# A graph layer on one core: where edge lists, the last chunk's attention and the experts' first rows stand in the queues

## The chip, the core and the metric

The kernel runs on one core of one Trainium2 chip. The metric is device time in microseconds (us): the median over runs of one compiled program. The profile is one further execution of the same program, taken by the hardware profiler. Names of engines: PE is TensorE, DVE VectorE, ACT ScalarE, POOL GpSimd, SP SyncE (it only issues transfers).

## What is computed

10,000 nodes with 512 features, 160,000 edges sorted by destination, all in float32:

```python
xn = layernorm(x)
h = relu(segment_sum((xn @ W)[src] * edge_weight[:, None], dst) + bias)
q, k, v = split(xn @ w_qkv.T)            # 8 heads of 64
q = softmax(q, over the head) * 64**-0.5
k = softmax(k, over all nodes)
context = k.T @ v                        # per head, 64 x 64
mix = layernorm((q @ context) @ w_out.T) * gamma
x = x + h + mix
xn = layernorm(x)
p = softmax(mean(xn) @ router.T)         # the top two of 11 set the weights of 6 experts
x = x + sum_e weight_e * (gelu(xn @ W1[e] + b1[e]) @ W2[e] + b2[e])
```

## The kernel before

The nodes go in 20 chunks: 19 of 512 rows (128 partitions by SUB = 4 rows) and a last one of 272 (68 partitions). The edges go in 1,250 tiles of 128; a group of four or eight tiles is gathered, weighted by a selection matrix and summed into one 128-row part.

PE's order is written out by hand. The orders of the other engines are made by a scheduler from the order of the code, the dependencies and a model of durations; within an engine, and within SP's line of transfers, that order is then fixed, so an instruction that waits holds all behind it. `behind(inst, other)` (L157) adds nothing but an edge for that scheduler.

Stages, in order of time:

1. Rows. `normal_rows` (L411) loads a chunk of `x` on SP, takes statistics on DVE, finishes them on POOL, scales on ACT and stores the normalised rows to `xn_d` from ACT. The first two chunks (KEPT) stay in SBUF; the others go through seven buffers (`a_io`). When LISTS = 10 chunks are normalised, the code asks for the four edge lists (`edges_listed`, L445) and begins `place_edges` (L454), a generator of some fifteen passes on DVE over the lists that works out each edge's place in its window. Two of its steps are taken after each further chunk, the rest at L858. Beside this PE works on the keys and queries of the first two chunks (EARLY = 2); `rows_of` (L830) reloads later chunks from `xn_d`, the first time for chunk 2.
2. Keys and edges. For each chunk, keys, queries and the context (`seven`, L246, and L911), with edge groups put in between. POOL gathers the messages (`edges_in`, L573: one indirect transfer of 256 KB per tile, 24 buffers), PE sums them (`edges_summed`, L595), ACT copies the sum out and stores it to `part_d`. `work` (L698) counts the time of PE's own products and calls for one tile per PACE = 0.9 us of it. POOL also adds parts of neighbouring windows in DRAM (`carry`, L672).
3. Rows again (L1062 to L1122). For chunk c: `attention` (L1038) of chunk c + 3 (loads `queries_in`, `rows_again`; products `po`; row statistics), the sums of the edges `gathered` (L1013, one indirect transfer on POOL) and transposed into `aT`, then the products `pg` and the rest of the row, stored to `x1_d`. The edge groups go on at one tile per ROW_PACE = 0.96 us; `far_enough` (L996) forces those that a chunk needs, with LEAD = 10 groups more. At c = 17 (NCH - 3) `all_edges_in` (L1005) sums what is left, closes the edges' buffers and asks for the experts' weights (`experts_weights`, L293); the attention of the last chunk, whose loads were issued at c = 16 and kept in `held["last"]`, comes after that. At c = 18 the rows of the experts' first chunk are asked for (`rows_in`, L315: four transfers), scaled on ACT (`normalising`, L341: 16 instructions) with statistics brought in place by `stats_of_squares` (L331, the product `pst`), transposed on DVE (`rows_turned`) and summed (`turned_in`).
4. Experts (L1370 to L1394): `hidden` and `rows_out` for 20 chunks, with products `px`, `py`, `pz`. A last branch, for more than four experts, is not taken with these inputs.

Of the kernel before, what the change touches and what calls it, by code (L numbers as in the profile page):

```python
# [9 lines left out]
F32 = mybir.dt.float32  # L10
# [17 lines left out]
FAR = 1.0e5  # L28
EARLY = 2
ROWS_IN = 1.6  # L30
LISTS = 10
CHECKED = 5
KEPT = 2
PRODUCT = 0.83
PACE = 0.9
ROW_PACE = 0.96
LATE = 4
MIXED = 3

# [3 lines left out]
CARRIES = [0, CHAINED] + [w for _, w in AT_HAND]  # L43
FIXED = 2
LAG = 16
LEAD = 10
LAG_ROWS = 10
AHEAD = 16
NORM2 = 7.0
# [7 lines left out]
def gps_layer_kernel(  # L57
# [41 lines left out]
    def tokens(t, c):  # L99
        b, r = chunks[c]  # L100
        return t[b : b + r * SUB, :].rearrange("(p s) d -> p s d", s=SUB)
# [55 lines left out]
    def behind(inst, other):  # L157

        tc.add_manual_dep(inst.ins, other.ins.name, mybir.DependencyInfo(
            mybir.DependencyClass.NoSync, mybir.DependencyReason.SCHED_ONLY), reason="order of work")  # L160
# [27 lines left out]
    def softmax_rows(q, r, s):  # L188

        q3 = q[:r, s, :].rearrange("p (h e) -> p h e", e=HEAD)  # L190
        qs = small.tile([P, D // HEAD], F32, name="qs")
        nc.vector.tensor_reduce(qs[:r], q3, axis=AX.X, op=ALU.add)
        nc.vector.reciprocal(qs[:r], qs[:r])
        nc.vector.tensor_tensor(q3, q3, qs[:r, :, None].to_broadcast([r, D // HEAD, HEAD]), ALU.mult)

    def transposed(o, t, r, psum, tag, by_act=(1, 3)):

# [190 lines left out]
    with ExitStack() as ph:  # L388
# [16 lines left out]


        normal = []
        placing = []
        last_stats = [None]

        def normal_rows(n):  # L411

            for c in range(len(normal), min(len(normal) + n, NCH)):
                r = chunks[c][1]
                xt = (xp if c < KEPT else a_io).tile([P, SUB, D], F32, name="xn")
                nc.sync.dma_start(xt[:r], tokens(x, c))
                mv = small.tile([P, SUB, 2], F32, name="mv")
                last_stats[0] = row_stats(xt, r, mv, on_pool=True)
                nc.gpsimd.tensor_tensor(mv[:r, :, 0], mv[:r, :, 0], mv[:r, :, 1], ALU.mult)
                nc.gpsimd.tensor_scalar(mv[:r, :, 0], mv[:r, :, 0], -1.0, None, op0=ALU.mult)  # L420
                for i in range(SUB):
                    nc.scalar.activation(xt[:r, i, :], xt[:r, i, :], AF.Identity,
                                         bias=mv[:r, i, 0:1], scale=mv[:r, i, 1:2])
                nc.scalar.dma_start(tokens(xn_d, c), xt[:r])
                normal.append(xt)
                if len(normal) == LISTS:
                    placing.append(place_edges(*edges_listed()))
                for _ in range(2 if placing else 0):
                    next(placing[0], None)

        zero = tmp.tile([P, D], F32, name="zero")
        nc.vector.memset(zero, 0.0)
# [21 lines left out]
        def place_edges(dst_sb, row_sb):  # L454


            nc.vector.tensor_scalar(row_sb, row_sb, 2, None, op0=ALU.arith_shift_right)
            yield
            nc.vector.memset(bases[:, 0:1], 0.0)
            nc.vector.memset(bases[:, NW:], FAR)  # L460
            nc.vector.tensor_copy(bases[:, 1:PAIRED],
# [34 lines left out]
            yield  # L496
            by_window_of(beyond, nodes, good, ALU.mult)
            yield
            nc.vector.scalar_tensor_tensor(place, place, float(SUB), good, op0=ALU.add, op1=ALU.subtract)
            yield  # L500
            nc.vector.scalar_tensor_tensor(good, place, float(SUB), beyond, op0=ALU.is_lt, op1=ALU.is_equal)
            yield
            nc.vector.scalar_tensor_tensor(good, place, float(WIN), good, op0=ALU.is_lt, op1=ALU.mult,
# [69 lines left out]
        def edges_in(i):  # L573

            t0, batch = tiles_of(i)
            n = min(GROUP * batch, NET - t0)
            m = [None] * n
            for j in range(batch):
                for h in range(GROUP):
                    k = h * batch + j  # L580
                    if k < n:
                        m[k] = pools["m"].tile([P, D], F32, name="msg")
                        nc.gpsimd.indirect_dma_start(  # L583
                            out=m[k], out_offset=None, in_=xn_d,
                            in_offset=bass.IndirectOffsetOnAxis(ap=src_sb[:, t0 + k : t0 + k + 1], axis=0))
            sel = pools["w"].tile([P, 2 * GROUP, WIN], F32, name="sel", bufs=6)
            if n < GROUP * batch:
                nc.vector.memset(sel[:, n:, :], 0.0)
            nc.vector.tensor_tensor(sel[:, :n], iota_w[:, None, :].to_broadcast([P, n, WIN]),  # L589
                                    place[:, t0 : t0 + n, None].to_broadcast([P, n, WIN]), ALU.is_equal)  # L590
            nc.vector.tensor_tensor(sel[:, :n], sel[:, :n],
                                    w_sb[:, t0 : t0 + n, None].to_broadcast([P, n, WIN]), ALU.mult)
            return batch, m, sel
# [236 lines left out]
        def rows_of(c):  # L830
            if c < KEPT:
                return normal[c]
            xn = xp.tile([P, SUB, D], F32, name="xn")
            nc.sync.dma_start(xn[: chunks[c][1]], tokens(xn_d, c))
            return xn

        def turned_rows(c, xn):
# [4 lines left out]
        def finish(o, ek, r, at):  # L842
            if o is ek:
                nc.vector.tensor_tensor(kacc[:r], kacc[:r], ek[:r, at, :], ALU.add)
            else:
                softmax_rows(o, r, at)

        wk = kvp.tile([P, KB, D], F32, name="wk")
        nc.sync.dma_start(wk, w_qkv_t[:, D : 2 * D].rearrange("(k p) d -> p k d", p=P))
# [5 lines left out]
        xnT = turned_rows(0, xn)  # L855
        for c, (_, r) in enumerate(chunks):
            if c == EARLY:
                for _ in placing[0]:  # L858
                    pass
                norm_ctx.close()  # L860
                pools["w"] = edge_ctx.enter_context(tc.tile_pool(name="edge_w", bufs=3))
                done[1] = -16 * PACE
                pools["m"] = edge_ctx.enter_context(tc.tile_pool(name="edge_m", bufs=24,
                                                                 reuse_waits="tile"))
# [37 lines left out]
                        finish(qt, ek, r, q)  # L902
            if c + 1 == EARLY:
                normal_rows(NCH)
                xn_next = rows_of(c + 1)
            if c + 1 < NCH:
                xnT = turned_rows(c + 1, xn_next)
# [97 lines left out]
        def all_edges_in():  # L1005
            edges_to(NQ)
            carry(CARRIES[-1], NW - 1)
            assert not carried
            pools.clear()
            edge_ctx.close()  # L1010
            experts_weights()

        def gathered(c):  # L1013
            r = chunks[c][1]
            n_rows = far_enough(c)
            at = io.tile([P, SUB, D], F32, name="at", tag="at" if c < NCH - 1 else "qT")
            nc.gpsimd.indirect_dma_start(
                out=at[:r].rearrange("p s d -> p (s d)"), out_offset=None, in_=by_four[: n_rows // SUB, :],
                in_offset=bass.IndirectOffsetOnAxis(ap=row_of[:r, c : c + 1], axis=0))
            return at  # L1020

        def queries_in(c):
            qT = io.tile([P, KB, SUB * P], F32, name="qT")
            nc.sync.dma_start(qT[:, :, : SUB * chunks[c][1]], qT_d[c])
            return qT

        def rows_again(c):
            xt = io.tile([P, SUB, D], F32, name="xt", bufs=1)
            nc.sync.dma_start(xt[: chunks[c][1]], tokens(x, c))
            return xt  # L1030
# [7 lines left out]
        def attention(c, beside):  # L1038


            r = chunks[c][1]
            qT, xt = held.pop("last") if c == NCH - 1 else (queries_in(c), rows_again(c))
            ot = io.tile([P, SUB, D], F32, name="ot", bufs=MIXED + 2)
            for s in range(SUB):
                if s == SUB - 1:
# [17 lines left out]
        for c, (_, r) in enumerate(chunks):  # L1063
# [2 lines left out]

            if c == NCH - 3:
                all_edges_in()
                ats += [gathered(c + 1), gathered(c + 2)]

            def nodes_rows():
                transposed(aT, at, r, psum, "ps", by_act=range(KB))

            if c + MIXED < NCH - 1:
                mixed.append(attention(c + MIXED, nodes_rows))
            elif c == NCH - 3:
                mixed.append(attention(NCH - 1, nodes_rows))
            else:
                nodes_rows()
            if c < NCH - 3:  # L1080
                ats.append(gathered(c + 1))
            if c == NCH - 4:
                held["last"] = queries_in(NCH - 1), rows_again(NCH - 1)

            for s in range(SUB):
                po = psum.tile([P, D], F32, name="pg", tag="ps")
# [20 lines left out]
            if c == NCH - 3:  # L1107
                sums_of_weights()
            if c == NCH - 2:
                io_f["in"] = ctx.enter_context(tc.tile_pool(name="f_in", bufs=1, reuse_waits="tile"))  # L1110

                io_f["squares"] = io_f["in"].tile([P, P // SQ, P], F32, name="squares")
                for b in range(P // SQ):
                    nc.vector.tensor_copy(
                        io_f["squares"][:, b].rearrange("k (g t) -> k g t", t=SQ),
                        ident[:, None, b * SQ : (b + 1) * SQ].to_broadcast([P, P // SQ, SQ]))
                xn = rows_in(0)
                st = small.tile([P, P // SQ, 1, SUB, 2], F32, name="st_sq", bufs=1)
                stats_of_squares(st, 0)
                for step in normalising(0, xn, st[:, :, 0]):  # L1120
                    step()
                turn = turned_in(0, rows_turned(0, xn))  # L1122
        in_order.close()
        query_ctx.close()

# [347 lines left out]
```

## Time and profile before

| what | value |
|---|---|
| median of 4 runs | 3517.76 us |
| lowest, highest | 3502.45, 3531.32 us |
| the profiled execution's own time | 3520.93 us |
| its span | 3519.2 us |
| PE busy | 3264.1 us, 93% of the span |
| PEld (weight loads) busy | 1918.3 us, 55% |
| DVE busy | 1766.5 us, 50% |
| ACT busy | 830.9 us, 24% |
| POOL busy | 1320.4 us, 38% |
| mean granted clock of PE | 0.964 |

The span is the time from the first to the last instruction of the profiled execution; 1.7 us of its own time lie around it. Busy time is the time in which an engine had an instruction running; a wait is given with what ended it (its releaser), as far as the trace shows one, and "issue" where it shows none. The granted clock is the share of PE's full clock that it was given.

### The profile page before, as it was taken

The numbers are of one execution on the slowest core, as the hardware profiler recorded it, in microseconds if no ns is written. First come the engines' busy times: TensorE is split into PE (matmuls) and PEld (weight loads), VectorE is DVE, ScalarE is ACT, GpSimd is POOL, SyncE is SP. The second block draws the span as 40 slices with busy tenths as digits, with TensorE's granted clock in tenths as the row PEclk, the third lists the DMA queues.
The fourth block names the chain that finished last, engine by engine and source line by source line (L and its number), as shares of the span: only waits on it lengthen the run. The fifth ranks groups of instructions, "written<-read, shape, count | busy, mean of one in ns | idle before, by whom it ended". The sixth has DMA issues, their size and how long they took to land. (4 is left out here: it accounts for less than half of the span.)

```text
span 3519.2 us, 36142 instructions
## 1 busy us (share of the span) xinstructions
PE 3264.1 (93%) x12819; PEld 1918.3 (55%) x12819; DVE 1766.5 (50%) x3902; ACT 830.9 (24%) x1674; POOL 1320.4 (38%) x1421
## 2 busy tenths in 40 slices
PE   6899998988989879998989987999999999999998
PEld 3343433333333333333333335888888888888886
DVE  6644545453444425555655566545445544544542
ACT  5321212121211112221212113222222222222221
POOL 3466666666666657666766730000000000000000
PEclk9999999999999979999999999999999999999999
DMA  9677777877777878898999892221212212122111
GB/s 389 236 224 247 228 247 243 262 218 222 229 219 240 253 260 317 300 321 294 336 309 318 302 265 63 60 72 60 60 48 84 56 52 84 49 60 72 60 37 38
DMA packets 216735, 654.39 MB, mean 186 GB/s; under 512 B 34425, under 2 KB 74361, under 8 KB 188831
## 3 DMA queue, kind: packets, MB, share of 16 engines
q0 software_dynamic: 104096, 354.29, 32.3%
q1 hardware_dynamic: 69992, 175.33, 15.2%
q10 hardware_dynamic: 42452, 122.31, 9.0%
q8 instruction: 105, 1.72, 0.2%
q14 instruction: 90, 0.74, 0.1%
HBM read 491.21 MB, written 166.63 MB: 187 GB/s over the span
## 5 line engine op out<-in xcount | busy, mean ns | idle before, releaser
L583 POOL DMA_INDIRECT msg<-xn_d,src_sb x1250 | 1239.3, 991 | 614.0 <-issue 285.1
L601 PE MATMUL pm<-msg,sel 128*32 128x512 f32 x2504 | 350.5, 613 | 40.0 <-issue 29.2
L911 PE MATMUL pc<-xn,ek 128*128 128x512 f32 (+1 forms) x640 | 311.2, 632 | 23.2 <-issue 17.5
L209 PE MATMUL pg<-wq,aT 128*128 128x512 f32 (+1 forms) x640 | 305.6, 622 | 19.8 <-issue 18.3
L209 PE MATMUL po<-G,qT 128*128 128x512 f32 (+1 forms) x640 | 302.4, 615 | 8.6 <-issue 7.9
L604 ACT COPY part<-pm 128x512 f32<-128x512 f32 x217 | 127.0, 586 | 723.1 <-remote 258.1
L209 PEld LDWEIGHTS pg<-wq,aT 128*128 128x128 f32 (+1 forms) x640 | 117.9, 193 | 208.0 <-issue 192.8
L601 PEld LDWEIGHTS pm<-msg,sel 128*32 128x32 f32 x2504 | 66.6, 109 | 290.1 <-issue 252.4
L911 PEld LDWEIGHTS pc<-xn,ek 128*128 128x128 f32 (+1 forms) x640 | 124.0, 201 | 183.3 <-issue 170.8
L209 PEld LDWEIGHTS po<-G,qT 128*128 128x128 f32 (+1 forms) x640 | 117.6, 192 | 184.5 <-issue 176.4
L243 PE MATMUL px<-xnT,w_sb 128*128 128x256 f32 (+1 forms) x800 | 203.9, 378 | 6.7 <-DVE u L1290 6.5
L166 DVE BATCH_NORM_STATS2 st<-ot 128x6 f32<-128x512 f32 (+1 forms) x160 | 110.3, 690 | 195.9 <-issue 111.4
L243 PE MATMUL p<-kq_sum,xs_b 128*128 128x512 f32 (+1 forms) x432 | 201.9, 600 | 3.3 <-issue 1.9
L243 PE MATMUL px<-w_sb,hh 128*128 128x256 f32 (+1 forms) x800 | 186.4, 380 | 0.0
L243 PE MATMUL py<-xs,w_sum 128*128 128x256 f32 (+1 forms) x800 | 185.9, 375 | 0.0
L243 PE MATMUL p<-wk,xnT 128*128 128x512 f32 (+1 forms) x288 | 149.2, 642 | 36.5 <-issue 29.2
L243 PE MATMUL py<-w_sum,hh 128*128 128x256 f32 (+1 forms) x800 | 179.2, 379 | 0.0
L589 DVE TENSOR_TENSOR sel<-iota_w,place 128x128 f32<-128x128 f32 (+2 forms) x217 | 74.3, 343 | 198.3 <-remote 71.4
L243 PEld LDWEIGHTS px<-xnT,w_sb 128*128 128x128 f32 x800 | 150.2, 191 | 29.7 <-DVE u L1290 10.0
L243 PEld LDWEIGHTS px<-w_sb,hh 128*128 128x128 f32 (+1 forms) x800 | 150.7, 188 | 23.0
L243 PEld LDWEIGHTS py<-w_sum,hh 128*128 128x128 f32 (+1 forms) x800 | 150.0, 188 | 22.7
L243 PEld LDWEIGHTS py<-xs,w_sum 128*128 128x128 f32 x800 | 150.2, 191 | 20.0
(298 smaller groups left out, 4574.2 us busy)
## 6 DMA issues: line engine op xcount, KB each, us to landing
part_d<-part ACTq DMA_DIRECT2D x217, 256.0 KB
msg<-xn_d,src_sb POOLq DMA_INDIRECT x1250
xn<-in_x SPq DMA_DIRECT2D x19, 1024.0 KB
xn_d<-xn ACTq DMA_DIRECT2D x19, 1024.0 KB
qT_d<-qT ACTq DMA_DIRECT2D x19, 1024.0 KB
qT<-qT_d SPq DMA_DIRECT2D x19, 1024.0 KB
xt<-in_x SPq DMA_DIRECT2D x19, 1024.0 KB
x_d<-ot SPq DMA_DIRECT2D x19, 1024.0 KB
```

Of the source, the lines that this page charges most:

```text
L166: nc.vector.bn_stats(st[:r, s, :], t[:r, s, :])
L209: nc.tensor.matmul(po[:r, :], t[:, kb, s * r : (s + 1) * r], w[:, kb, :], start=kb == 0, stop=kb == KB - 1)
L243: nc.tensor.matmul(o, lhs[j], rhs[j], start=start and j == 0, stop=stop and j == n - 1, skip_group_check=True)
L583: nc.gpsimd.indirect_dma_start(out=m[k], out_offset=None, in_=xn_d, in_offset=bass.IndirectOffsetOnAxis(ap=src_sb[:, t0 + k : t0 + k + 1], ...
L589: nc.vector.tensor_tensor(sel[:, :n], iota_w[:, None, :].to_broadcast([P, n, WIN]), place[:, t0 : t0 + n, None].to_broadcast([P, n, WIN]), ...
L601: nc.tensor.matmul(pm[h * WIN : (h + 1) * WIN, :], sel[:, k, :], m[k] if k < len(m) else m[0], start=j == 0, stop=j == batch - 1, skip_gro ...
L604: nc.scalar.copy(part, pm)
L911: nc.tensor.matmul(pc, ek[:r, s, cb * P : (cb + 1) * P], xn[:r, s, :], start=s == 0, stop=s == SUB - 1)
```

## The change

Seven edits in one:

- LISTS goes from 10 to 18; the steps of `place_edges` are no longer taken one by one after each chunk. Its first step is tied behind the last chunk's statistics, and the steps that return an instruction (the first, and the pass at L499) are tied behind the last softmax when the generator is run to its end.
- `rows_of` ties the first reload behind the last load of `x`.
- `gathered` ties the gather of a chunk's sums behind the last message asked for.
- ROW_PACE goes from 0.96 to 0.98, LEAD from 10 to 12.
- The last chunk's attention is no special case any more: it is done at c = 16, with its loads, and `held["last"]` is gone.
- At c = 17, when the edges are in, the experts' rows buffers are opened first, the first chunk's rows are asked for, then the weights.
- The copies `squares` move to the same place.

```diff
-LISTS = 10
+LISTS = 18
-ROW_PACE = 0.96
+ROW_PACE = 0.98
-LEAD = 10
+LEAD = 12
@@ softmax_rows
-        nc.vector.tensor_tensor(q3, q3, qs[:r, :, None].to_broadcast([r, D // HEAD, HEAD]), ALU.mult)
+        return nc.vector.tensor_tensor(q3, q3, qs[:r, :, None].to_broadcast([r, D // HEAD, HEAD]), ALU.mult)
@@ normal_rows
-                nc.sync.dma_start(xt[:r], tokens(x, c))
+                last_load[0] = nc.sync.dma_start(xt[:r], tokens(x, c))
...
-                for _ in range(2 if placing else 0):
-                    next(placing[0], None)
@@ place_edges
-            nc.vector.tensor_scalar(row_sb, row_sb, 2, None, op0=ALU.arith_shift_right)
-            yield
+            yield nc.vector.tensor_scalar(row_sb, row_sb, 2, None, op0=ALU.arith_shift_right)
...
-            nc.vector.scalar_tensor_tensor(place, place, float(SUB), good, op0=ALU.add, op1=ALU.subtract)
-            yield
+            yield nc.vector.scalar_tensor_tensor(place, place, float(SUB), good, op0=ALU.add, op1=ALU.subtract)
@@ edges_in
-                        nc.gpsimd.indirect_dma_start(
+                        held["asked"] = nc.gpsimd.indirect_dma_start(
@@ rows_of
-            nc.sync.dma_start(xn[: chunks[c][1]], tokens(xn_d, c))
+            load = nc.sync.dma_start(xn[: chunks[c][1]], tokens(xn_d, c))
+            if c == KEPT:
+                behind(load, last_load[0])
@@ finish
-                softmax_rows(o, r, at)
+                last_softmax[0] = softmax_rows(o, r, at)
@@ the loop over keys
-                for _ in placing[0]:
-                    pass
+                for step in placing[0]:
+                    if step:
+                        behind(step, last_softmax[0])
...
                 normal_rows(NCH)
+                behind(next(placing[0]), last_stats[0])
@@ all_edges_in
-            experts_weights()
@@ gathered
-            nc.gpsimd.indirect_dma_start(
+            sums = nc.gpsimd.indirect_dma_start(
...
+            behind(sums, held["asked"])
@@ attention
-            qT, xt = held.pop("last") if c == NCH - 1 else (queries_in(c), rows_again(c))
+            qT, xt = queries_in(c), rows_again(c)
@@ the loop over rows
             if c == NCH - 3:
                 all_edges_in()
+                io_f["in"] = ctx.enter_context(tc.tile_pool(name="f_in", bufs=1, reuse_waits="tile"))
+                rows_first = rows_in(0)
+                experts_weights()
+                io_f["squares"] = ...
                 ats += [gathered(c + 1), gathered(c + 2)]
...
-            if c + MIXED < NCH - 1:
+            if c + MIXED < NCH:
                 mixed.append(attention(c + MIXED, nodes_rows))
-            elif c == NCH - 3:
-                mixed.append(attention(NCH - 1, nodes_rows))
...
-            if c == NCH - 4:
-                held["last"] = queries_in(NCH - 1), rows_again(NCH - 1)
...
             if c == NCH - 2:
-                io_f["in"] = ...
-                io_f["squares"] = ...
-                xn = rows_in(0)
                 st = small.tile([P, P // SQ, 1, SUB, 2], F32, name="st_sq", bufs=1)
                 stats_of_squares(st, 0)
-                for step in normalising(0, xn, st[:, :, 0]):
+                for step in normalising(0, rows_first, st[:, :, 0]):
                     step()
-                turn = turned_in(0, rows_turned(0, xn))
+                turn = turned_in(0, rows_turned(0, rows_first))
```

More of the change, by code (lines that the diff above doesn't have):

```diff
@@ L407, in gps_layer_kernel @@
         normal = []
+        last_load = [None]
+        last_softmax = [None]
         placing = []
@@ L1068, in gps_layer_kernel @@
                 all_edges_in()
+                io_f["in"] = ctx.enter_context(tc.tile_pool(name="f_in", bufs=1, reuse_waits="tile"))
+                rows_first = rows_in(0)
+                experts_weights()
+                io_f["squares"] = io_f["in"].tile([P, P // SQ, P], F32, name="squares")
+                for b in range(P // SQ):
+                    nc.vector.tensor_copy(
+                        io_f["squares"][:, b].rearrange("k (g t) -> k g t", t=SQ),
+                        ident[:, None, b * SQ : (b + 1) * SQ].to_broadcast([P, P // SQ, SQ]))
                 ats += [gathered(c + 1), gathered(c + 2)]
@@ L1109, in gps_layer_kernel @@
             if c == NCH - 2:
[L1110 to L1116, printed above, removed]
-                xn = rows_in(0)
                 st = small.tile([P, P // SQ, 1, SUB, 2], F32, name="st_sq", bufs=1)
                 stats_of_squares(st, 0)
-                for step in normalising(0, xn, st[:, :, 0]):
+                for step in normalising(0, rows_first, st[:, :, 0]):
                     step()
-                turn = turned_in(0, rows_turned(0, xn))
+                turn = turned_in(0, rows_turned(0, rows_first))
         in_order.close()
```

## The prediction

> **What bounds the kernel now.** I read the stage windows first (columns: stretch, its length, then busy time of PE, PEld, DVE, ACT, POOL, the granted clock, DMA share, GB/s).
>
> ```profile
> 0.00:160.00 160.00, 114.59 (x337) 61.76 (x338) 105.01 (x299) 81.47 (x117) 51.81 (x102) 0.89 0.79 316
> 160.00:1273.00 1113.00, 1014.54 (x3673) 414.44 (x3671) 509.73 (x1030) 211.57 (x342) 728.88 (x742) 0.95 0.75 239
> 1273.00:2000.00 727.00, 668.03 (x2256) 250.03 (x2256) 399.49 (x1030) 147.84 (x284) 489.40 (x490) 0.95 0.89 309
> 2000.00:2075.00 75.00, 60.10 (x242) 21.41 (x235) 36.08 (x96) 14.82 (x30) 43.66 (x45) 0.91 0.88 289
> 2075.00:2200.00 125.00, 105.75 (x384) 61.62 (x383) 88.52 (x194) 40.03 (x91) 6.64 (x45) 0.94 0.44 109
> 2200.00:3519.00 1319.00, 1301.08 (x5940) 1109.05 (x5938) 627.66 (x1256) 335.15 (x812) 0.00 (x0) 1.00 0.20 60
> ```
>
> TensorE is the bound everywhere, and the change gives it the same matmuls. So only its idle time can be won: 45 us before 160, 99 while keys and edges run, 59 in the rows' stage, 15 where the edges end, 19 at the turn to the experts, 18 after. The PE timeline shows which of these the change touches (start, busy time, engine, line, operation; in brackets the idle time ahead and its releaser):
>
> ```profile
> 101.70 0.90 PE L201 MATMUL pt<-ident,qt 128*128 128x128 f32 x3 [13.55 <-DVE G L918]
> ...
> 2050.67 3.28 PE L601 MATMUL pm<-msg,sel 128*32 128x512 f32 x24
> 2061.97 1.94 PE L601 MATMUL pm<-msg,sel 128*32 128x512 f32 x8 [8.02 <-issue]
> 2066.59 3.64 PE L601 MATMUL pm<-msg,sel 128*32 128x512 f32 x16 [2.69 <-ACT part L604]
> 2070.17 11.43 PE L209 MATMUL po<-G,qT 128*68 128x512 f32 x24
> ...
> 2115.83 0.95 PE L337 MATMUL pst<-stats,squares 128*128 128x8 f32 x8
> ...
> 2145.26 1.19 PE L243 MATMUL px<-xs,w_sum 128*128 128x256 f32 x2 [13.68 <-DVE xs L235]
> ```
>
> Three holes: 13.55 us early, where DVE is behind; 10.7 us among the last edges, with 15 us of row work (the last chunk's `po`) standing right behind them; 13.68 us before the experts. What ends the last shows in the issues of SP and the instructions of ACT:
>
> ```profile
> 115.13 0.33 SPq L834 DMA_DIRECT2D xn<-xn_d  x1
> 115.56 0.54 SPq L416 DMA_DIRECT2D xn<-in_x  x1
> ...
> 2061.33 1.36 SPq L328 DMA_DIRECT2D xn<-x_d  x2
> 2071.61 14.15 SPq L305 DMA_DIRECT2D w_sb<-in_w  x16
> ...
> 2120.43 2.07 SPq L328 DMA_DIRECT2D xn<-x_d  x2
> ```
>
> ```profile
> 2117.18 1.25 ACT L203 COPY aT<-pt 128x272 f32<-128x272 f32 x4 [0.17 <-PE pt L201]
> ...
> 2134.20 0.20 ACT L174 ACTIVATE root<-ve 68x4 f32<-68x4 f32 x1 [11.06 <-DVE ve L169]
> 2134.52 6.26 ACT L351 ACTIVATE xn<-xn,st_sq 128x128 f32<-128x128 f32 x16
> ```
>
> Half of the experts' first rows is asked for at 2120, behind two stores, and their scaling (6.26 us, then a transpose of 2.31 and sums of 2.7 on DVE) starts only at 2134, behind the root of the very last chunk. And the gathers end so:
>
> ```profile
> 2061.80 0.95 POOL L583 DMA_INDIRECT msg<-xn_d,src_sb  x1 [0.30 <-issue]
> 2074.93 0.96 POOL L673 DMA_DIRECT2D part_d<-part_d  x1 [12.18 <-DMA w_sb<-in_w]
> 2079.99 1.42 POOL L1017 DMA_INDIRECT at<-part_d,row_of  x1 [4.11 <-DMA part_d<-part_d]
> ```
>
> **The early edits: -1.3 us.** In the built order the lists hardly move: `src` keeps its place on SP, the other three (625 KB each) let one row load past. The placing leaves DVE's stretch from 53 to 108. Its first part (passes of 9.8 us in all, 51 counts of 3.8; about 13 us) goes behind the last statistics, its second (L499 to L512: 1.43, 1.45, 1.43, 0.60, 1.06, 0.51, 0.92, a little less where they overlap: 7 us) behind the last softmax. The reload, which held the last row load (68 partitions) on SP from about 97, when its buffer was free, to 115.56, goes behind it.
> The hole at 101.70 ends when chunk 0's fourth softmax is done (103.2). Each softmax stands behind four statistics (2.4 us), and those wait for loads that land as before: DVE waited for one until 84.94. From there three groups of statistics, three softmaxes at 1.5 and a copy end at 98 to 100, so 3 to 5 us are won; I take 4. The first gather (150.42) comes some 20 us earlier, which is worth nothing: PE reaches its first edges at 184.76 without a wait, and POOL stops at its 24 buffers. Given back: the 7 us on DVE now stand ahead of `xs_b`, whose second sum was ready at 158.2 and which PE wants at 160.64. It comes to about 158.4 against 155.7: 2.7 us of new wait. The first 13 us run from about 114 to 127, where DVE had stood idle (13.63 us before 129.74); behind them are only `kacc` sums that nobody waits for yet. Bounds: gain 5; loss 5 (the 7 us uncovered, less 2).
>
> **Rows' stage: 0.** Pace 0.98 for 0.96 and lead 12 for 10 move edge groups between row products: 1184 tiles instead of 1192 are summed before the 16th chunk's transposes, 1212 and 1252 as before at the next two. 17 gathers of `at` go up to 32 messages later on POOL. Each still stands at least 20 messages ahead of its use, so no row waits for it; POOL loses some of its waits for them (26 us in all). But POOL has room: 28 messages at 1.25, one `at` and one carry make 37.5 us of a chunk's 43. PE's 59 idle us there are mostly "issue", ended by nothing that moves. Bounds: -15 (a quarter of it) to +10 (8 tiles at 1.25).
>
> **The edges' end: -14.1.** The last chunk's attention (its two loads, 16 products, 4 copies on ACT, its row statistics on DVE) moves from behind the edges to among them. From the 16th transposes (2000.42, less 8 tiles at 0.26 = 1998.3), PE has 5 x 3.47 of `po`, 68 x 0.26 of `pm`, 2 x 13.9 of `pg`, 1.9 of `pt`: 64.8, so 2063.1 without a wait. POOL had 42 messages left there. If the slower pace lets it stand at its 24 buffers, it again has 42, ends 2.1 earlier than 2062.75, and with the same 7.4 us to the last sum the edges end at 2068. If its lead stays 16 tiles it has 50: 2078. I take 2068, since the spare 5.5 us a chunk fill the buffers. Then two chunks at 15.8, and a wait: the `at` of chunk 18 needs the last part stored, the carry and the gather. Before, POOL's queue moved 1.2 MB between 2080 and 2092, so that chunk was in by about 2088, 17.8 after the last sum; cover is now 15.8, not 31. 2 us are lost. `pst` at 2068 + 31.6 + 2 = 2101.7 for 2115.83. Bounds: 2063 gives -19, 2078 gives -4.
>
> **The turn to the experts: -4.2.** All four loads (256 KB each) go ahead of the 17 weight loads and two stores on SP: they land some 30 us before `pst`. The weights are issued some 1.4 us later behind two more loads, which is covered: their first sum stood at 2097 and now stands behind `pst`. Three small loads on ACT (2.2 us of issue) stay where ACT is idle. On ACT 6 scalings, a root, 10 scalings now stand ahead of the last chunk's four `aT` copies. Counted from `pst`: scaling from 1.3, the root of chunk 18 in between (about 3.8), done at 7.8; `aT` 9.1; so PE waits 7.3 us ahead of its last `pg` (9.1 to 23.0). Beside it DVE transposes (10.8) and sums (14.2). The third sum of weights stands behind the fourth `pg` addition: 23.0 + 0.69 + 1.4 = 25.1, where `px` starts; it was 29.4. Bounds: 23.0 and 29.4.
>
> The row 2145 to 2149 shows a granted clock of 0.50 after the 13.7 us hole, 1.00 from 2152: about 2.5 us lost. [...]
>
> **Sum.** -1.3 - 14.1 - 4.2 = -19.6 on the profiled execution's 3520.9: 3501.3. The median of the four runs is 3.2 below that execution: 3498. The runs span 29 us, so about 1% (35 us) is what can be told from no change.
>
> **Rivals.** (a) The rows' stage gains too: with `at` later, POOL's waits and half of PE's 59 idle us go; with the best edge end and turn, -30 - 19 - 6: about 3465. For it: holes of 3 to 4 us on `pg` in that stage; against it: ACT sits idle in the same holes, so messages are not what is missing. (b) The edits don't do what they say: the early one gains nothing, the edges stay bound by POOL (2078) and the turn gives 2: 3512. For it: the lists' order on SP. (c) Slower: POOL starves the end. With 12 tiles of lead lost, 64 to 68 messages remain at 1998, 85 us and carry and two gathers: the edges end at 2092, `pst` at 2126, and with early loss 5 the time is about 3525. It decides from a lead of about 4 tiles (edges after 2087). For it: more edges are left late; against it: POOL's spare 5.5 us a chunk. (d) Gain in place, but a late stall in the rows' stage of 8 or more tiles of several chunks: 3555 and more.
>
> **How the numbers follow.** Forecast 0.55 (3485 to 3512), (a) 0.12, (b) 0.15, (c) 0.13, (d) 0.05. Low 3470 (near (a)), high 3530 ((c) and half the spread of runs). Faster by over 1% (under 3482.6): most of (a) and a bit of the forecast's edge, 0.12; slower (over 3552.9): (d), 0.06; same 0.82.
>
> **What would show it.** Hole at 88 to 101.7 shrinking to about 10, a new wait of 2 to 3 at the first `p` from `kq_sum`; no wait over 3 us among the last `pm`; `pst` near 2100; 7 us ahead of the last `pg`; under 3 ahead of `px`. Wrong if POOL's last gather falls after 2066, or if the rows' stage changes its 43 us a chunk.

## The result and the profile after

The changed kernel took 3532.91 us, median of 35 runs (3511.15 to 3556.41), the kernel before 3515.95 us in the runs beside it. The ratio of the fast runs (one of the kernel before took 6927.71 us and is not among them) is 1.0044, 95% interval 1.0031 to 1.0058: slower by 0.44%, within 1%. The forecast was 3498 us, with a range of 3470 to 3530. The profiled execution took 3534.09 us (span 3532.3; before 3520.93 and 3519.2).

The stage windows of the changed kernel (columns as above):

```profile
0.00:160.00 160.00, 115.83 (x340) 62.63 (x341) 105.48 (x297) 82.18 (x117) 41.90 (x96) 0.91 0.79 319
160.00:1273.00 1113.00, 1012.83 (x3599) 411.94 (x3598) 506.52 (x1020) 209.79 (x340) 716.05 (x735) 0.95 0.74 232
...
2075.00:2200.00 125.00, 99.70 (x368) 57.79 (x369) 77.40 (x181) 38.62 (x89) 7.11 (x45) 0.87 0.49 132
```

In the second stretch fewer instructions were begun (3599 of PE for 3673): the first transposes of `at` come 17 us later (1369.24 for 1352.05). In the last row shown PE was busy 6 us less, at a lower clock (0.87 for 0.94). Its timeline shows where:

```profile
96.50 0.90 PE L201 MATMUL pt<-ident,qt 128*128 128x128 f32 x3 [8.47 <-DVE G L920]
...
158.63 3.75 PE L243 MATMUL p<-kq_sum,xs_b 128*128 128x512 f32 x4 [4.29 <-DVE xs_b L228]
...
2076.93 5.31 PE L599 MATMUL pm<-msg,sel 128*32 128x512 f32 x24 [8.07 <-ACT part L602]
...
2109.54 3.52 PE L201 MATMUL pt<-ident,at 128*128 128x128 f32 x16 [11.66 <-DMA at<-part_d,row_of]
...
2126.64 0.95 PE L337 MATMUL pst<-stats,squares 128*128 128x8 f32 x8
...
2134.78 16.58 PE L209 MATMUL pg<-wq,aT 128*68 128x512 f32 x32 [6.14 <-ACT aT L203]
2154.21 2.05 PE L243 MATMUL px<-xs,w_sum 128*128 128x256 f32 x4 [2.85 <-DVE w_sum L228]
```

Read it against the timeline of before. The early hole shrank from 13.55 to 8.47, and 4.29 came back as a new wait; the first edges' sum starts at 185.40 for 184.76. The last sum of edges ends at 2082.2 for 2070.2, with 15 us less row work behind it. The `at` of chunk 18 is waited for 11.66 us, where there was no wait. From `pst` to `px` it is 27.57 us for 29.43. What POOL did at the edges' end:

```profile
2072.57 0.95 POOL L581 DMA_INDIRECT msg<-xn_d,src_sb  x1 [0.30 <-issue]
2090.27 0.96 POOL L671 DMA_DIRECT2D part_d<-part_d  x1 [16.75 <-DMA xn<-x_d]
2098.45 1.04 POOL L1018 DMA_INDIRECT at<-part_d,row_of  x1 [7.22 <-DMA part_d<-part_d]
```

Its last message goes out 10.8 us later (2061.80), the carry 15.3 later, and the carry takes 8.2 us to the next gather where it took 5.1. Counted from the end of the last sum, that chunk's `at` is in after 27.3 us; the forecast took 17.8.

Between the first transposes of `at` and `pst` this one execution is 6.4 us shorter than the one before; its loss stands ahead of that (17 us) and, to 4 us, behind `px` (1378.1 us to the end for 1373.94). Executions of one kernel spread over 42 to 45 us here, so one pair can't say what is spread; the experiments split the change instead.

### The profile page after: what moved, and what is told of

It is laid out like the page before. It is cut to its first block, busy times and chain, and to the rows that moved or that the text cites. A ratio compares the mean times of both kernels' runs of the same rounds, so it can differ in the third digit from the quotient of the medians.

```text
span 3532.3 us, 36132 instructions
## 1 busy us (share of the span) xinstructions
PE 3278.8 (93%) x12819; PEld 1924.5 (54%) x12819; DVE 1769.1 (50%) x3902; ACT 831.5 (24%) x1674; POOL 1306.9 (37%) x1421
## 5 line engine op out<-in xcount | busy, mean ns | idle before, releaser
L599 PE MATMUL pm<-msg,sel 128*32 128x512 f32 x2504 | 359.6, 617 | 39.7 <-issue 27.0
L913 PE MATMUL pc<-xn,ek 128*128 128x512 f32 (+1 forms) x640 | 308.7, 626 | 21.3 <-issue 14.1
L243 PEld LDWEIGHTS py<-xs,w_sum 128*128 128x128 f32 x800 | 149.8, 191 | 19.9
```

What stands on the lines that cost most here:

```text
L243: nc.tensor.matmul(o, lhs[j], rhs[j], start=start and j == 0, stop=stop and j == n - 1, skip_group_check=True)
L599: nc.tensor.matmul(pm[h * WIN : (h + 1) * WIN, :], sel[:, k, :], m[k] if k < len(m) else m[0], start=j == 0, stop=j == batch - 1, skip_gro ...
L913: nc.tensor.matmul(pc, ek[:r, s, cb * P : (cb + 1) * P], xn[:r, s, :], start=s == 0, stop=s == SUB - 1)
```

## The experiments

The runs fell on four chips: e1 to e4 on one (number 3), e5 to e8 on a second (11), e9 to e12 on a third (13), e13 to e18 on a fourth (0). The chip of the result above is not on record. The kernel before took 3302, 3302 and 3299 us on the first three, and on the fourth 3520 beside e13 to e15 and 3539 beside e16 to e18. Every ratio is to runs of the kernel before on the same chip beside it; times and profiles of different chips are set side by side only among the first three, where the kernel before takes the same time, and in the last section. *Cover* is the row work on PE that stands between the last sum of edges and the first use of what follows from it.

**e1, the early edits alone** (lists at 18, reload tied, placing tied).

```diff
-LISTS = 10
+LISTS = 18
...
+                behind(load, last_load[0])
...
+                        behind(step, last_softmax[0])
...
+                behind(next(placing[0]), last_stats[0])
```

> The kernel before with the early edits alone (reload behind the last row load, edge lists after 18 chunks, placing tied behind the last statistics and the last softmax). Theory A (the loss is at the edges' end, the early edits trade a shorter hole against a new wait): ratio to the kernel before 0.999 to 1.001; hole near 100 us about 8.5 instead of 13.55, first pm within 2 us of 184.8, and the stretch from there to the last chunk's transposes about 966 us long, as before. Theory B (the early edits are the loss: the 15 us more that the key and edge stage took in the profile after belong to them): ratio 1.003 to 1.005 and that stretch near 981 us.

0.9996 (0.9987 to 1.0004). The hole is 9.18 us, for 13.07 in the kernel before (e6, on chip 11); the new wait is 4.28; from the first sum of edges to the first transposes of `at` it is 1002.8 us for 1002.1. No gain or loss is told from nothing here, and theory B's 15 us do not show on this chip.

**e2, the rows' edits alone.**

```diff
-ROW_PACE = 0.96
+ROW_PACE = 0.98
-LEAD = 10
+LEAD = 12
...
+            behind(sums, held["asked"])
```

> The kernel before with the rows' stage edits alone (pace 0.98, lead 12, gathers of at behind the messages asked for before them). Theory A: the 21 us that the rows' stage was shorter in the profile after are partly real, ratio 0.995 to 0.999, the stage from the first to the sixteenth transposes of at near 630 us instead of 648; a little of it lost again behind the edges, where 8 more tiles are left. Theory C (that difference is the spread of one execution): ratio 0.999 to 1.002, stage 640 to 655.

1.0027 (1.0015 to 1.0038): some 9 us slower, against both theories. Its explanation needs a profile of the kernel before where that takes 3302 us (e6).

**e3, the last chunk's attention in its turn, alone.**

```diff
-            qT, xt = held.pop("last") if c == NCH - 1 else (queries_in(c), rows_again(c))
+            qT, xt = queries_in(c), rows_again(c)
...
-            elif c == NCH - 3:
-                mixed.append(attention(NCH - 1, nodes_rows))
...
```

> The kernel before with the last chunk's attention in its turn, no longer kept behind the edges; weights and first rows as before. Theory A: the edges end about 12 us later with the row work that covered them gone, and the wait for the at of chunk 18 comes to 2 to 8 us (part store, carry, gather, beside the weight loads only): pst within 5 us of before, ratio 0.999 to 1.002. Rival D (the wait for at has nothing to do with the first rows' loads): the same wait as in the changed kernel, 11 to 12 us, ratio 1.002 to 1.004.

0.9995 (0.9985 to 1.0004), as theory A expected. The wait for `at` is there, and shorter than rival D has it; `pst` comes at 1893.10, in e6 at 1893.02, so what the wait costs, the earlier row work gives back:

```profile
1875.18 3.65 PE L201 MATMUL pt<-ident,at 128*128 128x128 f32 x16 [6.10 <-DMA at<-part_d,row_of]
```

**e4, the experts' first rows asked for at the edges' end, alone**, the last attention kept behind the edges.

```diff
             if c == NCH - 3:
                 all_edges_in()
+                rows_first = rows_in(0)
+                experts_weights()
...
-                xn = rows_in(0)
```

> The kernel before with the experts' first rows asked for at the edges' end ahead of the weights; the last chunk's attention kept behind the edges as cover. Theory A (contention of these loads with part store, carry and gather): the at of chunk 18 lands some 27 us after the last pm as in the changed kernel instead of 18, but the 15 us of po and 16 of pg hide it; the distance from pst to px falls from 29.4 to 27 to 28; ratio 0.999 to 1.000. Rival D: at lands some 18 us after the last pm, as before.

0.9967 (0.9957 to 0.9977): 9 (by the medians) to 11 us (by the ratio) faster, more than expected. There is no wait for `at`, and `px` starts 24.74 us after `pst`, without a wait, where it was 29.43. That is 4.7 us; where the rest of the gain lies, the profiles don't show.

**e5, the whole change where the kernel before takes 3302 us.** No edit.

> The changed kernel itself beside its parts, since the four parts multiply to 0.9985 while the first comparison of the whole gave 1.0044. If the parts simply add: ratio 0.997 to 1.000. Theory A (the last chunk's attention was the cover of the chain part store, carry, gather, and the first rows' loads lengthen that chain; neither costs by itself, together they do): ratio 1.001 to 1.005, and ahead of the at transposes of chunk 18 a wait of 8 to 12 us, where the kernel with the attention edit alone had 6.10 and the one with the first rows alone none.

1.0032 (1.0020 to 1.0044). The four parts multiply to 0.9985, so they do not simply add; the ratio and the wait are those that theory A expected:

```profile
1889.43 3.34 PE L201 MATMUL pt<-ident,at 128*128 128x128 f32 x16 [9.97 <-DMA at<-part_d,row_of]
```

**e6, the kernel before, for its profile.** No edit.

> The kernel before, for its profile beside those of the parts. If the 15 us by which the key and edge stage and the 21 us by which the rows' stage differed in the first two profiles are the spread of executions, its stages match those of the kernel with the early edits alone within 3 us; POOL's last message is issued within 2 us of 1845, some 8 us ahead of the kernel with the rows' edits alone (1853.01).

The key stage is as in e1 (1002.1 us for 1002.8), and POOL's last message goes out at 1840.53. The first lines are of e6, the second of e2 (POOL's last message, then PE at the sixteenth chunk's transposes, in each):

```profile
1840.53 0.95 POOL L583 DMA_INDIRECT msg<-xn_d,src_sb  x1 [0.31 <-PE pm L601]
1765.55 1.97 PE L201 MATMUL pt<-ident,at 128*128 128x128 f32 x16
```

```profile
1853.01 0.94 POOL L583 DMA_INDIRECT msg<-xn_d,src_sb  x1 [0.30 <-issue]
1764.85 1.97 PE L201 MATMUL pt<-ident,at 128*128 128x128 f32 x16
```

PE reaches that chunk at the same time in both, but POOL has then 50 messages left in e6 and 61 in e2 (counted in its timeline; the expectations give those issued, a few of them counted twice). The last message is 12.5 us later, ten times 1.25, and `pst` 16 us later (1909.11 for 1893.02); by the ratio 9 of these belong to the edits. A chunk takes 38.6 us here; the 37.5 us that a chunk needs of POOL leave one to spare. POOL's gaps of more than 0.4 us in the fifteen chunks ahead of that point add up to 15.5 us in e6 and 34.3 in e2. What fills them is not shown. It is not the buffers: at each message at most 13 of the 24 hold one that is not yet summed, in e2 as in e6. The DMA engines are busy to 0.97 in that stage of e6 (in e7, to nine tenths or more in every slice of the page from 1239 to 1734 us, at 340 to 354 GB/s) and to 0.90, at 315 GB/s, in that of the first profile of before, so the transfers, and not POOL's issuing, may be the limit here; no run tells the two apart.

**e7, the changed kernel without the rows' edits.**

```diff
-ROW_PACE = 0.98
+ROW_PACE = 0.96
-LEAD = 12
+LEAD = 10
...
-            behind(sums, held["asked"])
```

> The changed kernel without the rows' stage edits (pace 0.96, lead 10, gathers of at not tied). Theory E (the slower pace is the larger loss: fewer tiles summed in the rows' stage, so POOL's last message is issued later and everything behind the edges with it): ratio 0.995 to 0.998, faster than the whole by 7 to 10 us. Theory A alone (all the loss is the wait for at): as the whole, within 3 us of it, ratio 1.000 to 1.004.

1.0002 (0.9993 to 1.0010), 9.0 us ahead of the whole: the rows' edits again cost what e2 showed. The wait for `at` is still there (11.04), so theory A holds beside E, and neither alone gives this ratio: without the wait this kernel should be near e8.

**e8, early edits and first rows, cover kept.** e1 and e4 together.

> The early edits and the first rows asked for at the edges' end, the last chunk's attention kept behind the edges, pace and lead as before. If the two gains add, ratio 0.995 to 0.997 (some 11 to 14 us), no wait ahead of the at transposes of chunk 18, pst to px 24 to 25 us. If the early edits are worth nothing, 0.9967 as with the first rows alone.

0.9972 (0.9961 to 0.9983), 11 us ahead of e7, which differs by the last chunk's attention alone. That edit costs nothing alone (e3) and 0.3% beside the early first rows. The two profiles show a part of it in place: from the sixteenth chunk's transposes to `px` e7 takes 152.7 us and e8 148.8; another 8 us lie ahead of them (1775.10 and 1766.81), where the edit changes none of PE's work, and may be spread. The turn (PE, then DVE's last sum for `px`):

```profile
1891.34 0.95 PE L337 MATMUL pst<-stats,squares 128*128 128x8 f32 x8
...
1899.48 16.30 PE L209 MATMUL pg<-wq,aT 128*68 128x512 f32 x32 [6.14 <-ACT aT L203]
1915.62 1.03 PE L243 MATMUL px<-xs,w_sum 128*128 128x256 f32 x4
```

```profile
1908.06 0.68 DVE L236 TENSOR_TENSOR xs<-xnT,xs 128x512 f32<-128x512 f32 x1
```

DVE has the sums ready at 1908.7, so `px` starts when the last `pg` ends.

**e9, the pace alone**, and **e10, lead and tie alone**: the lines of e2's diff, taken apart.

> The kernel before with the row pace 0.98 for 0.96 alone. Theory E (tiles summed later leave POOL's 24 buffers full, so it issues that many messages later): some 12 messages fewer issued when the sixteenth chunk's transposes begin (1217 in the kernel before, 1204 with all rows' edits), last message 8 to 13 us later, ratio 1.002 to 1.004. Theory F (the gathers of at moved behind the messages hold POOL up): ratio 0.999 to 1.001 here, and the loss with lead and tie.

> The kernel before with lead 12 and the gathers of at behind the messages asked for before them, pace 0.96 kept. Theory E: ratio 0.999 to 1.001, 1214 to 1219 messages issued when the sixteenth chunk's transposes begin. Theory F: ratio 1.002 to 1.004 and the last message 8 to 13 us later.

The pace: 1.0021 (1.0012 to 1.0031); 59 messages left at the sixteenth chunk (50 in e6), the last at 1851.78, the numbers that theory E expected. Its reason, full buffers, is not in the trace: at most 13 of 24 are taken here too. Lead and tie: 1.0031 (1.0019 to 1.0043), with 51 left there, but that chunk reached 11 us later (1776.55), and the last message at 1851.10; so F's numbers came as well. How that loss arises is not shown: e7, with neither lead nor tie, reaches that chunk at 1775.10, so the 11 us of one profile may be spread. The two do not add up (e2 has both, 1.0027).

**e11, the changed kernel without the rows' edits, weights late**: `experts_weights()` moved behind the store of chunk 17.

```diff
                 rows_first = rows_in(0)
-                experts_weights()
...
             if c == NCH - 3:
+                experts_weights()
                 sums_of_weights()
```

> The changed kernel without the rows' edits, and with 16 of the 17 weight loads behind the store of the chunk whose rows follow the edges, so that they are not under way beside part store, carry and gather. Contention (these loads lengthen the chain): the wait ahead of the at transposes of chunk 18 falls from 11.04 to 4 to 7 us, pst some 5 us earlier; the weights' sums may then hold px by up to as much, ratio 0.998 to 1.001. If the chain is only serial (it takes what it takes, beside any load): the wait stays at 10 to 12 us, ratio 1.000 to 1.004.

0.9976 (0.9967 to 0.9985), 0.26% better than the ratio of e7 (on chip 11), which differs by the place of these loads alone (15 of 176 KB and one of 2,816: 5.5 MB; the first of the 17 stays ahead). First e7, then e11 (POOL's carry and gather, and the PE row that waits for it):

```profile
1863.01 0.96 POOL L671 DMA_DIRECT2D part_d<-part_d  x1 [13.09 <-DMA b_sb<-in_b_a]
1870.57 1.03 POOL L1018 DMA_INDIRECT at<-part_d,row_of  x1 [6.61 <-DMA part_d<-part_d]
1883.06 3.64 PE L201 MATMUL pt<-ident,at 128*128 128x128 f32 x16 [11.04 <-DMA at<-part_d,row_of]
```

```profile
1858.78 0.96 POOL L671 DMA_DIRECT2D part_d<-part_d  x1 [13.41 <-DMA b_sb<-in_b_a]
1863.72 1.03 POOL L1018 DMA_INDIRECT at<-part_d,row_of  x1 [3.98 <-DMA part_d<-part_d]
1870.12 1.94 PE L201 MATMUL pt<-ident,at 128*128 128x128 f32 x16 [2.28 <-DMA at<-part_d,row_of]
```

From the gather's issue to PE's use it is 12.5 us with the weights under way and 6.4 without; the carry shrinks from 7.6 to 4.9. Both waits end when the `at` lands, and from the end of the last sum that is 26.7 us in e7 and 17.9 in e11. This is contention: the serial chain was to leave the wait at 10 to 12 us. Part of the gain is given back, since the sums of weights now stand later on DVE (`px` 30.17 us after `pst`).

**e12, e8 with the pace turned the other way.**

```diff
-ROW_PACE = 0.96
+ROW_PACE = 0.94
```

> The early edits and the first rows asked for early, cover kept, with the pace turned the other way: 0.94 for 0.96. Theory E: some 12 more messages issued at the sixteenth chunk's transposes, the last one 5 to 12 us earlier, ratio to the kernel before 0.994 to 0.997, so 0 to 10 us ahead of the same kernel at 0.96 (3291.80). If POOL is already at one message in 1.25 us through the whole stage, the pace changes nothing: 0.996 to 0.998.

0.9987 (0.9978 to 0.9996): no gain over e8 (0.9961 to 0.9983). Fewer messages are left at the sixteenth chunk (42 for 50), but in this profile that chunk comes 13 us later and the last message at the same time (1841.60 for 1841.62). Theory E's gain did not come. The faster pace put more sums ahead of the rows, and the last message went out no sooner; that it holds the rows back rests on this one profile.

**e13, the tie alone**, and **e14, lead 12 alone**; **e17, the tie once more**.

> The kernel before with the gathers of at tied behind the messages asked for before them, lead 10 and pace 0.96. Lead and tie together gave 1.0031 with the rows' stage some 11 us longer. If the tie alone is the cause (a gather of at stands later on POOL, and the messages behind it later): ratio 1.002 to 1.004 and the sixteenth chunk's transposes 6 to 12 us later than the 1765.55 of the kernel before. If it is the lead: 0.999 to 1.001.

> The kernel before with lead 12 for 10 alone. If the lead is the cause (each gather of at asks for two tiles more to be summed ahead of it, so TensorE takes up messages that have not landed yet): ratio 1.002 to 1.004, waits of the sums for messages near 21 us in the stage as with lead and tie together, against 13.3 in the kernel before. If it is the tie: 0.999 to 1.001.

> The kernel before with the gathers of at tied behind the messages, alone, once more: on the chip where the kernel before takes 3520 us it gave 1.0002 with 0.0019 either way, too wide for what lead and tie together cost where it takes 3300 (1.0031). Where POOL has no spare time (3300): tie at fault, 1.002 to 1.004; lead at fault, 0.999 to 1.001. Where it has (3520): 0.998 to 1.002 by both.

e13 1.0002 (0.9983 to 1.0021) and e14 1.0001 (0.9985 to 1.0017), where the kernel before takes 3520 us; e17 1.0026 (1.0002 to 1.0051) where it takes 3539, outside the 0.998 to 1.002 expected there and barely clear of nothing. None ran where the kernel before takes 3300 us and e10 lost 0.31%, so which of the two cost it there stays open.

**e15 and e16, the changed kernel without the rows' edits, weights issued by POOL** behind the gathers.

```diff
                 ats += [gathered(c + 1), gathered(c + 2)]
+                experts_weights()
...
-                nc.sync.dma_start(w1_sb[g * SQ : (g + 1) * SQ, j, :], ...)
+                nc.gpsimd.dma_start(w1_sb[g * SQ : (g + 1) * SQ, j, :], ...)
```

> The changed kernel without the rows' edits, with 16 of the 17 weight loads issued by POOL behind the two last gathers of at, instead of by SP ahead of them. Contention: the wait ahead of the at transposes of chunk 18 stays near 2.3 us as with the weights late on SP (11.04 with them early), and since these loads now begin some 11 us sooner than there, the sums of weights no longer hold px: pst near 1886, px 24 to 26 us behind it; ratio 0.994 to 0.997, the fastest so far. If loads of weights beside the gathers lengthen them even when issued behind them: wait of 6 to 11 us, ratio 0.998 to 1.001.

> The changed kernel without the rows' edits and with 16 weight loads issued by POOL behind the gathers of at, once more, since the first comparison left 0.9964 to 1.0015: the wait for at was 3.44 us and pst to px 24.58 there, as contention says. If these two are worth at the end what they are in place (some 11 us of px against the kernel before, 8 of the wait and 5 of the turn less 2 given back): 0.995 to 0.998. If something else takes them back: 0.999 to 1.001.

POOL issues all 17 loads here. In place both halves came, in e15's PE timeline:

```profile
2097.95 3.56 PE L201 MATMUL pt<-ident,at 128*128 128x128 f32 x16 [3.44 <-DMA at<-part_d,row_of]
...
2115.08 0.95 PE L337 MATMUL pst<-stats,squares 128*128 128x8 f32 x8
...
2139.66 1.03 PE L243 MATMUL px<-xs,w_sum 128*128 128x256 f32 x4
```

3.44 us of wait and 24.58 from `pst` to `px` (3.54 and 23.55 in e16). At the end little is left: 0.9990 (0.9964 to 1.0015) and 0.9991 (0.9972 to 1.0011). This is the second case of e16's expectation, that something else takes the gain back; what it is stays open.

**e18, e8's kernel beside e16.**

> Early edits and first rows asked for early, cover kept (0.9972 where the kernel before takes 3300 us), beside the kernel with weights issued by POOL on the same chip. If keeping the cover and taking the loads out of the way are two ways to the same end: both within 0.0015 of each other, 0.995 to 0.998.

1.0001 (0.9982 to 1.0019), with `px` 24.94 us after `pst` and no wait for `at`. So the two are within 0.0015, but 0.995 to 0.998 failed for both.

**What stays open.** Where the kernel before takes 3302 us, the change is split: 1.0002 without the rows' edits, 1.0032 with them, and 0.9972 without rows' edits and attention. There the fastest versions are the first rows alone (0.9967), e8 (0.9972) and e11 (0.9976), not told apart. Where it takes 3520 or 3539 us, no version but e17 was told apart from the kernel before. There PE waits in the key stage for nothing that the profile shows, as the waits of the first profile of before have it (releaser, total us, times, longest):

```profile
PE p L243 <- issue: 31.1, 14, 5.2
PE pc L911 <- issue: 17.5, 19, 3.2
```

In e6 PE was idle for 1.1 of the 910 us from 160 to 1070. The first transposes of `at` came at 1352.05, 1360.76 and 1352.61 in three profiles without the early edits (3516 and 3520 us), at 1369.24 and 1363.87 in two with them; at 1374.91 without, 1380.61 and 1384.60 with (3539). That would be 8 to 11 us lost to the early edits where the kernel before takes over 3500 us, as much as e4 gained on chip 3. But three profiles without them differ by 9 us themselves, and they were not run alone there, so it is not shown. For the same reason the 17 us by which the first pair differs ahead of the rows' stage have no shown cause.

## Why the prediction failed, step by step

- **Early edits, -1.3: not told from nothing on the chip of e1** (-1.3 us, interval -4.3 to +1.3 by the ratio; that the middle is the forecast is luck). The path was right, the price of the wait was not: forecast were 4 us of the hole won and 2.7 lost ahead of `p`; 5.1 and 4.29 came in the first pair, 3.9 and 4.28 in e1 beside e6. Where the kernel before takes 3520 us it stays open, as said.
- **Rows' stage, 0: wrong, within its bounds.** The failed step is "But POOL has room: 28 messages at 1.25, one `at` and one carry make 37.5 us of a chunk's 43". The 43 was PE's time with its unexplained waits and a mean clock of 0.95 in it. Where these are absent a chunk takes 38.6 us, and the edits cost 9 us (e2, e5 against e7). What takes POOL's time there is open (e6). Nor did its lead over the sums grow at 43: in the profile after (41.8 us a chunk) 50 messages were left at the sixteenth chunk's transposes (1996.76), which is a lead of 16 tiles, where the forecast chose 42 left and had 50 as the other end. Its last sum then ended at 2082, near the 2078 of that end and 14 us behind the 2068 that the forecast took.
- **The edges' end, -14.1: wrong.** "cover is now 15.8, not 31. 2 us are lost" named the right wait and mis-sized it: 11.66, 9.97, 11.04 in three profiles. With the late last sum, `pst` came at 2126.64 and not at 2101.7. The 17.8 us of the chain were an estimate from a kernel whose first rows came later, and after its 31 us of cover no wait could show what the chain takes. From the last sum to the use of the `at`, in the kernels that wait for it, it took 27.3, 25.6 and 26.7 us with first rows and weights beside it (after, e5, e7), 21.7 with the weights alone (e3), 19.9 and 20.9 with the weights behind the gathers (e15, e16), and 17.9 with the weights late (e11): the chain's length goes with what runs beside it. From its issue to PE's use the gather of `at` alone took 12.5 us with SP's weight loads beside it and 6.4 without (e7, e11).
- **The turn, -4.2: -1.9 in the changed kernel.** Its path was as forecast: PE waits for `aT` (8.1 us from `pst`, 9.1 forecast), and the weights' sums stand on DVE behind the last `pg` addition, so that `px` waits 2.85 us behind the last `pg` (2.1 forecast). What was missing is the half clock (next point). Where the cover is kept the turn came near the 25.1 forecast (24.28 in e8, 24.74 in e4), but with luck: there DVE has the sums ready early, which takes off the 2.1, and the half clock adds 2.4 in e8 (the last `pg` 16.30 for 13.90, at a granted clock of 0.50 from 1899 to 1903 and 0.90 to 1909).
- **The half clock in the last `pg`, not in the sum: 2.7** (16.58 for 13.90; granted clock 0.50 from 2134 to 2138, 0.74 to 2142, then 1.00). It is not hidden: in e8 the last `pg` takes 16.30 and `px` starts at its end, and in the changed kernel DVE waits for this `pg` ahead of the sums. The loss behind the hole ahead of `px`, about 2.5 us in the prediction, went in part: from `px` to its third product it is 6.7 us for 7.9. And the wait for `at` has a half clock of its own that nobody counted: behind its 11.66 us the transposes take 3.52 us where they took 1.91, at a granted clock of 0.52 from 2109 to 2113. In e11, where PE waited only 2.28, they take 1.94.
- **The rivals.** Nearest is (c), a slower end by lost lead of POOL. It needed the last sum past 2087; that came at 2082, and the wait for `at` added the rest. Its own numbers add up to about 3528, not 3525. (b) had the edges bound by POOL, which came, but not the wait. (a) and (d) did not come. The forecast's sign of being wrong, a last message of POOL after 2066, came: 2072.57.

## What to carry to other kernels

Work that stands behind the last of a stage may be the cover of a chain that shows no wait; before moving it, write out the whole chain (here store, carry, gather) with its own duration, and ask which new transfers run beside it. An edit that is free alone can cost beside another: the last attention's move was free alone and cost 0.3% beside the early loads. A wait on PE cost more than its own length here: behind 11.66 us of it the next transposes took 3.52 us where they took 1.91 without a wait. An engine's spare time per step is to be measured against the step without its stalls, since the stalls were not the same on every chip here.

## What was not expected of the hardware

The same program, on one core, took 3299 to 3302 us on three chips, 3520 and 3539 on a fourth, and 3516 on that of the result. The difference lies ahead of the experts, most of it in the key and edge stage: the first transposes of `at` came at 1185.70 in e6 and at 1352.05 in the first profile of before, with PE idle 98 us of a stretch of 1113 in the slower, at a mean clock of 0.95, and 1.1 us of one of 910 in the faster, at 1.00 (over the whole execution 0.964 and 0.987). From `px` to the end it was 1373.35 and 1373.94. What makes the one slower is not shown. Edits worth 0.3% on the first three chips could mostly not be told from nothing on the fourth.
